# First attention: tokens as the stationary side of the scores, the mask added by VectorE

## The chip, the cores and the metric

The kernel runs on one core of a Trainium2 chip. A core has TensorE (matmuls and transposes into PSUM), VectorE, ScalarE and GpSimd for elementwise work, SyncE, and queues that start DMA transfers. The profile calls them PE, DVE, ACT, POOL and SP, and PEld is TensorE's loading of a stationary operand. The metric is the device time of one execution in microseconds (us). Before the change it is 703.99 us, the median of three runs (702.55 to 706.32).

## The reference, cut to what matters

Four batches of 1024 tokens of width 256 (x), with 77 context rows per batch, go through two layers of gated cross-attention and feed-forward. The change is in the first attention alone:

```python
def xattn(hidden, keys, values, mask):
    scores = einsum('bqd,bkd->bqk', hidden, keys)
    scores = where(mask[:, None, :] == 0, NEG_INF, scores)
    weights = softmax(scores, axis=2)
    return einsum('bqk,bkd->bqd', weights, values)

x = x + tanh(g_xattn[0]) * xattn(layernorm(x), context, context, mask)
x = x + tanh(g_ffn[0])   * (top-2 of 8 experts + shared expert)(layernorm(x))
x = x + tanh(g_xattn[1]) * second_attention(layernorm(x), context)   # softmax over the tokens
x = x + tanh(g_ffn[1])   * (gated feed-forward with int8 weights)(layernorm(x))
```

The kernel leaves layernorm out of the scores' input: since softmax doesn't change when a constant is added to a row, it uses the raw x, context rows with their mean taken off, and multiplies by the token's 1/sigma inside the exponential.

## The kernel before, in words

**Blocks.** The 4096 tokens are eight blocks `n` of 512 (two per batch), each of four token tiles of 128. The first part of the kernel works block by block in named steps. `sa:n` takes the statistics of x on VectorE (L303, L304, L306; GpSimd makes the power, L308). `a2:n` transposes x on TensorE (L333) and copies it to SBUF, one half by ScalarE and one by VectorE (L340). `context:b` takes the mean off the context rows of a batch (L265 to L269), transposes them (L272) and copies them to `cT` (L275). `a3:n` makes the scores. `a4:n` takes each token's maximum (L391, L399) and the exponentials (L403). `a5:n` transposes the probabilities (L417) and copies them (L419). `a6:n` multiplies by the context (L432) and adds to x (L438). Then come the statistics of the result (`sb`), the normalized rows on ScalarE (`nb`, L321), their transposes (`b2`), router logits (`b3`, L463), routing, ranks, and the shared expert.

**The scores before.** `a3` holds 77 context rows stationary and moves 512 tokens past them, so the scores come out with the context on the partitions (`scT`, 77 x 512). ScalarE copies them out, multiplying by 0 or 1 per context row and adding 0 or a large negative number (L379, tile `scs`). `a4` then transposes the four token tiles back on TensorE (L387), into a PSUM tile `sc` that stays taken until the four exponentials have read it.

**What sets the order.** `FIRST` is a hand-written list of steps, performed from left to right; TensorE, VectorE and ScalarE each run their instructions in exactly that order. A `.` takes the next piece of the shared expert's matmuls (L846 up, L906 down; a finished pair is evicted by ScalarE's Silu L860 and VectorE's L863), a `~` is a matmul whose result is never read (L288), a `,` starts two scatters on GpSimd (L576). The stretch around the first blocks reads

```
~ ~ ~ . ~ . ~ . ~ . . ~ sa:0 ~ a2:0 ~ context:0 ~ , sa:1 . sa:2 ~ zeros:0 a3:0 ~ ~ , a2:1 a4:0
a3:1 sa:3 a5:0 a4:1 ~ a6:0 a5:1 . a2:2 a2:3 a6:1 sb:0 context:1 nb:0 ~ biases:0 a3:2 sb:1 b2:0
a4:2 a3:3 . . . nb:1 a4:3 , a5:2 sa:4 . . . . . sa:5 . , b2:1
```

and later `weights:0 . . a3:4 a3:5 nb:2 gates:0 . a4:4 ranks:0 sb:3 . , a4:5` and `sb:4 . . nb:4 sb:5 a3:6 a3:7 . . gates:1 . a4:6`. Afterwards the routed experts run (L735 to L783), and the list `SECOND` runs the second layer.

**Tiles and loads.** PSUM has three pools: `up` (four banks: scores of `a3`, logits, shared expert, unread matmuls), `dn` (two) and `tp` (two: all transposes). SP's queue loads x in parts (L142, L145, L148), the context of batch 0 (L143) and of batches 1 to 3 (L149); ACT's queue loads the mask (L144) and the two pairs of gates (L146, L147), whose tanh (L251) is the first thing that ScalarE does.

Of the kernel before, what the change touches and what calls it, by code (L numbers as in the profile page):

```python
# [9 lines left out]
F32 = mybir.dt.float32  # L10
F32R = mybir.dt.float32r
I32 = mybir.dt.int32
U32 = mybir.dt.uint32
AF = mybir.ActivationFunctionType
ALU = mybir.AluOpType
# [3 lines left out]
P = 128  # L19
B, S, D = 4, 1024, 256  # L20
SK = 77
DC = D // P
NT = S // P
BLK = 512
TB = BLK // P
# [23 lines left out]
NEG = -(2.0**100)  # L49
# [29 lines left out]
def kernel(  # L79
# [34 lines left out]
    nc = tc.nc  # L114
    const = ctx.enter_context(tc.tile_pool(name="const", bufs=1))
# [5 lines left out]
    work = ctx.enter_context(tc.tile_pool(name="work", bufs=7))  # L121
    small = ctx.enter_context(tc.tile_pool(name="small", bufs=2))
    ps_up = ctx.enter_context(tc.tile_pool(name="ps_up", bufs=4, space=PSUM))
    ps_dn = ctx.enter_context(tc.tile_pool(name="ps_dn", bufs=2, space=PSUM))
    ps_tp = ctx.enter_context(tc.tile_pool(name="ps_tp", bufs=2, space=PSUM))

    ident = const.tile([P, P], F32, name="ident")
# [6 lines left out]


    cv = work.tile([SK, B, D], F32, tag="cv", name="cv", bufs=1)
    mask_i = const.tile([SK, B], I32, name="mask_i")
    tg_in = const.tile([P, 4], F32, name="tg_in")
    gw = const.tile([P, DC, E], F32, name="gw")
    gb = const.tile([P, 1, E], F32, name="gb")  # L140
    cv_in = context.rearrange("b k d -> k b d")
    nc.sync.dma_start(xs[0][:, : NT // 2], x_v[0][:, : NT // 2])  # L142
    nc.sync.dma_start(cv[:, 0], cv_in[:, 0])  # L143
    nc.scalar.dma_start(mask_i, mask.rearrange("b k -> k b"))  # L144
    nc.sync.dma_start(xs[0][:, NT // 2 :], x_v[0][:, NT // 2 :])  # L145
    nc.scalar.dma_start(tg_in[:, 0:2], g_xattn.partition_broadcast(P))  # L146
    nc.scalar.dma_start(tg_in[:, 2:4], g_ffn.partition_broadcast(P))  # L147
    nc.sync.dma_start(xs[1], x_v[1])  # L148
    nc.sync.dma_start(cv[:, 1:], cv_in[:, 1:])  # L149
    nc.sync.dma_start(gw, gate_w)  # L150
    nc.sync.dma_start(gb[:, 0], gate_b.partition_broadcast(P))

# [5 lines left out]
    for g in range(SH):  # L158
        for sb, src, n in zip((ws1_sb, ws3_sb, ws2_sb), (ws1, ws3, ws2), ("ws1", "ws3", "ws2")):
            t = wp.tile([P, 2, EI], F32, tag=f"{n}_{g}", name=f"{n}_{g}")  # L160
# [91 lines left out]
    tg_x0, tg_x1, tg_f0, tg_f1 = (tg[:, i : i + 1] for i in range(4))  # L252


    m01 = const.tile([SK, B], F32, name="m01")
    nc.vector.tensor_scalar(m01, mask_i, 0.0, None, ALU.not_equal)
    neg = const.tile([SK, B], F32, name="neg")
    nc.vector.tensor_scalar(neg, m01, 1.0, -NEG, ALU.subtract, ALU.mult)


    cT = const.tile([P, DC, B * SK], F32, name="cT")
# [86 lines left out]
    xT_a, score, prob, probT, ln = {}, {}, {}, {}, {}  # L348
# [16 lines left out]
    def a3(n):  # L365


        b, blk = blocks[n]
        scT = ps_up.tile([P, BLK], F32, tag="up", name=f"scT{n}")
        for dc in range(DC):  # L370
            nc.tensor.matmul(  # L371
                scT[:SK],
                lhsT=cT[:, dc, b * SK : (b + 1) * SK],
                rhs=xT_a[b][blk][:, dc],
                start=(dc == 0),
                stop=(dc == DC - 1),
            )
        score[n] = work.tile([SK, BLK], F32, tag="t2k", name=f"scs{n}")
        nc.scalar.activation(  # L379
            score[n], scT[:SK], AF.Identity, bias=neg[:, b : b + 1], scale=m01[:, b : b + 1]  # L380
        )

    def a4(n):
        scs = score.pop(n)
        sc = ps_tp.tile([P, BLK], F32, tag="tp", name=f"sc{n}")
        for tt in range(TB):
            nc.tensor.transpose(  # L387
                sc[:, tt * SK : (tt + 1) * SK], scs[:, tt * P : (tt + 1) * P], ident[:SK, :SK]
            )
        nmx = small.tile([P, TB], F32, tag="nmx", name=f"nmx{n}")  # L390
        nc.vector.tensor_reduce(  # L391
            nmx,
            sc[:, : TB * SK].rearrange("p (t k) -> p t k", k=SK),
            AX.X,
            ALU.max,
            negate=True,
        )
        rs = ln.pop(("a", n))[0]
        nc.vector.tensor_mul(nmx, nmx, rs)  # L399
        pr = work.tile([P, TB, SK], F32, tag="pr", name=f"pr{n}", bufs=2)  # L400
        sm = small.tile([P, TB], F32, tag="sm", name=f"sm{n}", bufs=4)
        for tt in range(TB):
            nc.scalar.activation(  # L403
                pr[:, tt],
                sc[:, tt * SK : (tt + 1) * SK],
                AF.Exp,
                bias=nmx[:, tt : tt + 1],
                scale=rs[:, tt : tt + 1],
                accum_out=sm[:, tt : tt + 1],
            )  # L410
        prob[n] = pr, sm
# [813 lines left out]
    def last_weights(_):  # L1225
# [6 lines left out]
        "last": last_weights,  # L1232
        "context": context_T, "zeros": lambda _: zero_rest(),
        "biases": halves_of_biases, "a2": a2, "a3": a3, "a4": a4, "a5": a5, "a6": a6,
        "b2": b2_and_shared, "b3": b3_, "routing": routing, "weights": weights,
        "ranks": ranks, "gates": gates_turned, "fetch": lambda i: combine(i // 2, i % 2),
# [104 lines left out]
```

## Time and profile before

| | us |
|---|---|
| median of three runs | 703.99 |
| the profiled execution, time | 705.87 |
| the profiled execution, span | 704.2 |
| PE busy (share of the span) | 665.7 (95%) |
| DVE busy | 382.4 (54%) |
| ACT busy | 284.4 (40%) |
| POOL busy | 276.6 (39%) |
| L371 scores, PE, 32 records | 17.7 busy |
| L387 transposes of the scores, PE, 32 records | 3.6 busy |
| L379 copy with mask, ACT, 8 | 6.1 busy |

The profile shows one execution. Its time is 1.67 us longer than its span, which begins and ends with the core's own instructions. A matmul of 32-bit floats appears as two records. Records of one engine overlap at their ends, so the distance from one start to the next, as the chain of waits gives it, says more than the length of one. The chain of waits goes back from the last instruction to what released it; the share of an engine in it is the part of the span in which nothing but that engine could have been faster. The timeline gives for each group of instructions its start, its time, and in brackets how long the engine had been idle before it and what ended that.

### The profile page before, as it was taken

The numbers are of one execution on the slowest core, as the hardware profiler recorded it, in microseconds if no ns is written. First come the engines' busy times: TensorE is split into PE (matmuls) and PEld (weight loads), VectorE is DVE, ScalarE is ACT, GpSimd is POOL, SyncE is SP. The second block draws the span as 40 slices with busy tenths as digits, with TensorE's granted clock in tenths as the row PEclk, the third lists the DMA queues.
The fourth block names the chain that finished last, engine by engine and source line by source line (L and its number), as shares of the span: only waits on it lengthen the run. The fifth ranks groups of instructions, "written<-read, shape, count | busy, mean of one in ns | idle before, by whom it ended". The sixth has DMA issues, their size and how long they took to land.

```text
span 704.2 us, 9788 instructions
## 1 busy us (share of the span) xinstructions
PE 665.7 (95%) x2996; PEld 495.8 (70%) x2996; DVE 382.4 (54%) x1096; ACT 284.4 (40%) x570; POOL 276.6 (39%) x309
## 2 busy tenths in 40 slices
PE   7689999999998999999999999999999899799896
PEld 4447487567644888888888888757767678567685
DVE  5767667566494433333343333246667559568544
ACT  1361722633221132323323233054466674666642
POOL 2111471466571133433333333231563535643642
PEclk9989999999999999999999999999999899999999
DMA  6700020121166566776776762671160004300001
GB/s 223 271 2 1 35 93 1 40 88 56 72 222 224 179 234 218 238 260 219 250 257 225 247 230 81 129 135 30 46 121 30 1 30 90 60 31 31 1 31 60
DMA packets 42259, 84.38 MB, mean 120 GB/s; under 512 B 8079, under 2 KB 12855, under 8 KB 41823
## 3 DMA queue, kind: packets, MB, share of 16 engines
q1 hardware_dynamic: 32704, 58.05, 25.0%
q0 software_dynamic: 8896, 25.70, 13.3%
q8 instruction: 24, 0.39, 0.2%
q14 instruction: 28, 0.23, 0.1%
q10 hardware_dynamic: 607, 0.00, 0.0%
HBM read 57.77 MB, written 26.87 MB: 120 GB/s over the span
## 4 chain that ended last, share of the span: by engine, by line
PE 79%; DVE 11%; ACT 5%; issue 3%; DMA 1%; POOL 1%; DVEq 0%; ACTq 0%; POOLq 0%
PE y_r L772 9%; PE pa_r L750 9%; PE pc_r L750 9%; PE y_s L906 8%; PE pa_s L846 6%; PE pc_s L846 6%; PE pa_f L1105 5%; PE pc_f L1105 5%; PE yT_f L1135 4%; PE pt_r L735 2%; PE scT L371 2%; PE sq L1014 2%; PE pl L463 2%; PE pc L1048 2%; PE pv L432 1%
## 5 line engine op out<-in xcount | busy, mean ns | idle before, releaser
L783 POOL DMA_INDIRECT yg<-yr,rowplace x74 | 72.3, 977 | 154.0 <-ACT yr L781 141.1
L1119 POOL TENSOR_TENSOR hh<-h_f,hm_f 128x512 fp32r<-128x512 f32 x47 | 63.5, 1357 | 70.2 <-DVE hm_f L1115 51.1
L762 DVE SCALAR_TENSOR_TENSOR hr<-pc_r,bt,sr 128x256 f32<-128x256 f32 (+7 forms) x78 | 32.3, 455 | 83.2 <-PE pc_r L750 83.2
L576 POOL DMA_INDIRECT xg<-rows,place x64 | 62.5, 977 | 23.0 <-issue 14.7
L772 PE MATMUL y_r<-rows_and_weights,hr 128*128 128x256 f32 (+5 forms) x296 | 70.3, 380 | 0.0
L750 PE MATMUL pa_r<-xrT,rows_and_weights 128*128 128x256 f32 (+7 forms) x312 | 69.4, 365 | 0.3 <-DVE xrT L740 0.3
L781 ACT ACTIVATE yr<-y_r,rowat 128x256 f32<-128x256 f32 (+4 forms) x74 | 31.2, 470 | 94.1 <-PE y_r L772 94.1
L750 PE MATMUL pc_r<-xrT,rows_and_weights 128*128 128x256 f32 (+7 forms) x312 | 69.1, 364 | 0.0
L846 PE MATMUL pa_s<-xnT_b,ws 128*128 128x512 f32 x128 | 62.7, 598 | 0.7 <-ACT s_s L860 0.5
L1105 PE MATMUL pa_f<-xp,ws_last 128*128 128x512 f32 x192 | 57.8, 420 | 5.7 <-POOL xp L1080 4.7
L846 PE MATMUL pc_s<-xnT_b,ws 128*128 128x512 f32 x128 | 61.8, 596 | 0.0
L750 PEld LDWEIGHTS pc_r<-xrT,rows_and_weights 128*128 128x128 f32 x312 | 56.5, 190 | 6.6
L772 PEld LDWEIGHTS y_r<-rows_and_weights,hr 128*128 128x128 f32 (+5 forms) x296 | 54.4, 186 | 8.8 <-issue 0.7
L1135 PE MATMUL yT_f<-hh,ws_last 128*128 128x512 f32 x192 | 55.9, 413 | 3.7 <-ACT hh L1123 3.0
L906 PE MATMUL y_s<-ws,hT 128*128 128x256 f32 x256 | 58.5, 380 | 0.0
L750 PEld LDWEIGHTS pa_r<-xrT,rows_and_weights 128*128 128x128 f32 x312 | 53.9, 190 | 5.7 <-DVE xrT L740 0.6
L1112 DVE SCALAR_TENSOR_TENSOR h_f<-pc_f,s_f 128x512 f32<-128x512 f32 x48 | 33.1, 689 | 38.6 <-PE pc_f L1105 19.6
L1105 PE MATMUL pc_f<-xp,ws_last 128*128 128x512 f32 x192 | 53.6, 402 | 0.3 <-DVE vw L1043 0.3
L906 PEld LDWEIGHTS y_s<-ws,hT 128*128 128x128 f32 x256 | 48.7, 191 | 7.2 <-issue 0.5
L761 ACT ACTIVATE sr<-pa_r,bt 128x256 f32<-128x256 f32 (+7 forms) x78 | 31.2, 451 | 54.5 <-PE pa_r L750 54.5
L1105 PEld LDWEIGHTS pa_f<-xp,ws_last 128*128 128x128 f32 x192 | 36.8, 194 | 17.5 <-POOL xp L1080 6.6
L740 DVE COPY xrT<-pt_r 128x512 f32<-128x512 f32 (+7 forms) x39 | 25.0, 643 | 43.1 <-PE pt_r L735 43.1
(246 smaller groups left out, 1091.2 us busy)
## 6 DMA issues: line engine op xcount, KB each, us to landing
rows_and_weights<-in_w_dram SPq DMA_DIRECT2D x117, 256.0 KB, 4.3
rows_and_weights<-xg SPq DMA_DIRECT2D x32, 272.0 KB
x<-yg POOLq DMA_DIRECT2D x16, 512.0 KB, 5.9
xg<-zero_row SPq DMA_DIRECT2D x16, 272.0 KB, 3.7
out_dram<-x SPq DMA_DIRECT2D x7, 512.0 KB, 2.6
x<-in_x_dram SPq DMA_DIRECT2D x3, 1024.0 KB
ws<-in_ws_dram SPq DMA_DIRECT2D x6, 256.0 KB, 5.7
yg<-yr,rowplace POOLq DMA_INDIRECT x74, 4.3
```

The costliest lines, as they stand in the source:

```text
L576: disjoint("xg", nc.gpsimd.indirect_dma_start(out=xg, out_offset=bass.IndirectOffsetOnAxis(ap=place[:, k, t], axis=0), in_=rows[b][:, t], ...
L750: nc.tensor.matmul(o[:, ic], lhsT=wa[:, dc, ic * P : (ic + 1) * P], rhs=xrT[:, dc], start=(dc == 0), stop=(dc == DC - 1),)
L761: nc.scalar.activation(s, ps[0][:, ic], AF.Silu, bias=bt[:, 0, ic, j])
L762: nc.vector.scalar_tensor_tensor(hr[:, ic], ps[1][:, ic], bt[:, 1, ic, j], s, ALU.add, ALU.mult)
L772: nc.tensor.matmul(o[:, tt], lhsT=hr[:, ic, tt * n : (tt + 1) * n], rhs=w[2][:, ic], start=(ic == 0), stop=(ic == IC - 1),)
L783: disjoint("yg", nc.gpsimd.indirect_dma_start(out=yg, out_offset=bass.IndirectOffsetOnAxis(ap=place[:, tt : tt + 1], axis=0), in_=y[:, tt] ...
L846: nc.tensor.matmul(ps[name], lhsT=w[g][:, dc, ic * P : (ic + 1) * P], rhs=xnTs[b][blk][:, dc], start=(dc == 0), stop=(dc == DC - 1),)
L906: nc.tensor.matmul(o[:, j], lhsT=hTs[n][i // IC][:, i % IC, cols], rhs=ws2_sb[i // IC][:, i % IC], start=False, stop=(j == 1 and i == SH * ...
L1105: nc.tensor.matmul(o, lhsT=w[:, dc, cols], rhs=halved[n][:, dc, part], start=(dc == 0 and part == 0), stop=(dc == DC - 1 and part == 1),)
L1112: nc.vector.scalar_tensor_tensor(h, pc, SCALE, s, ALU.mult, ALU.mult)
L1119: (nc.vector if end else nc.gpsimd).tensor_tensor(hh[:, 1], h, hm, ALU.subtract)
L1135: nc.tensor.matmul(y, lhsT=wd_sb[GO[i // IC]][:, i % IC, dc * P : (dc + 1) * P], rhs=hh[:, part], start=(i == 0 and part == 0), stop=(i == ...
```

## The change

`a3` now holds 128 tokens stationary and moves the 77 context rows past them: eight matmuls (four token tiles by two halves of the width) in place of two. The scores come out with the tokens on the partitions. VectorE adds the mask, broadcast over the partitions and the four tiles, and writes SBUF. The transposes in `a4` are gone, and its maximum and exponentials read SBUF. The mask is loaded once to every partition (128 x 308 integers), and one instruction makes the addend. SP's queue loads the context of batches 1 to 3 ahead of x of batch 1. The lists of steps are the same.

```diff
-    mask_i = const.tile([SK, B], I32, name="mask_i")
+    mask_i = const.tile([P, B * SK], I32, name="mask_i")
...
-    nc.scalar.dma_start(mask_i, mask.rearrange("b k -> k b"))
+    nc.scalar.dma_start(mask_i, mask.rearrange("b k -> (b k)").partition_broadcast(P))
...
+    nc.sync.dma_start(cv[:, 1:], cv_in[:, 1:])
     nc.sync.dma_start(xs[1], x_v[1])
-    nc.sync.dma_start(cv[:, 1:], cv_in[:, 1:])
...
-    m01 = const.tile([SK, B], F32, name="m01")
-    nc.vector.tensor_scalar(m01, mask_i, 0.0, None, ALU.not_equal)
-    neg = const.tile([SK, B], F32, name="neg")
-    nc.vector.tensor_scalar(neg, m01, 1.0, -NEG, ALU.subtract, ALU.mult)
+    neg = const.tile([P, 1, B * SK], F32, name="neg")
+    nc.vector.tensor_scalar(neg[:, 0], mask_i, 0.0, NEG, ALU.is_equal, ALU.mult)
...
-        scT = ps_up.tile([P, BLK], F32, tag="up", name=f"scT{n}")
-        for dc in range(DC):
-            nc.tensor.matmul(
-                scT[:SK],
-                lhsT=cT[:, dc, b * SK : (b + 1) * SK],
-                rhs=xT_a[b][blk][:, dc],
-                start=(dc == 0),
-                stop=(dc == DC - 1),
-            )
-        score[n] = work.tile([SK, BLK], F32, tag="t2k", name=f"scs{n}")
-        nc.scalar.activation(
-            score[n], scT[:SK], AF.Identity, bias=neg[:, b : b + 1], scale=m01[:, b : b + 1]
-        )
+        sc = ps_up.tile([P, BLK], F32, tag="up", name=f"sc{n}")
+        for tt in range(TB):
+            for dc in range(DC):
+                nc.tensor.matmul(
+                    sc[:, tt * SK : (tt + 1) * SK],
+                    lhsT=xT_a[b][blk][:, dc, tt * P : (tt + 1) * P],
+                    rhs=cT[:, dc, b * SK : (b + 1) * SK],
+                    start=(dc == 0),
+                    stop=(dc == DC - 1),
+                )
+        score[n] = work.tile([P, BLK], F32, tag="t2k", name=f"scs{n}")
+        nc.vector.tensor_tensor(
+            score[n][:, : TB * SK].rearrange("p (t k) -> p t k", k=SK),
+            sc[:, : TB * SK].rearrange("p (t k) -> p t k", k=SK),
+            neg[:, :, b * SK : (b + 1) * SK].to_broadcast([P, TB, SK]),
+            ALU.add,
+        )
 
     def a4(n):
-        scs = score.pop(n)
-        sc = ps_tp.tile([P, BLK], F32, tag="tp", name=f"sc{n}")
-        for tt in range(TB):
-            nc.tensor.transpose(
-                sc[:, tt * SK : (tt + 1) * SK], scs[:, tt * P : (tt + 1) * P], ident[:SK, :SK]
-            )
+        sc = score.pop(n)
```

## The prediction, made before the changed kernel ran

> **What bounds the kernel now.** I read the page first, then the chain of waits stage by stage, then the timeline and the granted clock where the chain leaves TensorE. On the page:
>
> ```profile
> PE 665.7 (95%) x2996; PEld 495.8 (70%) x2996; DVE 382.4 (54%) x1096; ACT 284.4 (40%) x570; POOL 276.6 (39%) x309
> PE 79%; DVE 11%; ACT 5%; issue 3%; DMA 1%; POOL 1%; DVEq 0%; ACTq 0%; POOLq 0%
> ```
>
> TensorE is busy for 95% of the span and carries 79% of the chain. So what leaves TensorE's order counts, unless the next thing in that order has to wait anyway. The change touches only the first 140 us. There the chain of waits has these pieces (start, length):
>
> ```profile
> 1.85 8.51 DMA tg_in<-in_g_ffn_dram
> ...
> 37.99 3.17 PE scT L371 x4
> ...
> 74.15 3.43 PE scT L371 x8
> ...
> 78.88 0.28 PE sc L387 x4
> ...
> 92.90 3.46 PE y_s L906 x16
> ...
> 97.23 1.69 PE pl L463 x16
> ```
>
> The start hangs on the gates' load. One block's scores are four records and take 1.72 us at full clock (3.43 for two) but 3.17 at 38 us; its back-transposes take 0.28. The y_s and pl rows serve to price the new matmuls. The clock behind the 3.17 is in the last column but two of the windows:
>
> ```profile
> 34.00:37.00 3.00, 0.49 (x3) 0.52 (x4) 2.19 (x9) 0.00 (x0) 1.01 (x1) 0.50 0.44 149
> 37.00:40.00 3.00, 3.00 (x5) 1.18 (x5) 2.67 (x12) 2.07 (x4) 0.00 (x0) 0.50 0.00 0
> ```
>
> TensorE idles from 32.0 to 36.5 us and is then granted half clock until 40.6; VectorE meanwhile is busy for 2.2 and 2.7 of 3 us. So up to 36.5 the chain is VectorE's. The timeline shows two places where TensorE waits for ScalarE (start, length, idle before):
>
> ```profile
> 52.11 1.13 PE L846 MATMUL pa_s<-xnT_b,ws 128*128 128x512 f32 x2
> 87.41 1.13 PE L846 MATMUL pa_s<-xnT_b,ws 128*128 128x512 f32 x2 [0.55 <-ACT s_s L860]
> ```
>
> Both are the first shared-expert matmul for which no PSUM bank is free until ScalarE has finished exponentials, loaded another table and done one Silu (s_s). At 52.11 the weight load in front of it had also waited for s_s, though TensorE itself lost only about 0.1 us. These two, and the similar pc_s at 138.07 (s_s from 137.52), decide what a shorter TensorE order is worth.
>
> **Part 1: the matmuls.** The new block has 16 records of 128 columns loaded and 77 streamed. Here a rule speaks against the change. The Trainium skill, "TensorE: Matmul & The Clock Gate", section "Part 3: Packing small matmuls — row/col tiling" (The mechanism), says that weight loads overlap matmuls in flight "only when row_grp differs", and all of these use the full array; with the same page's 128/1.2 = 107 ns per load ("LDWEIGHTS (loading the stationary operand)") and 77/512 of scT's 430 ns per record, 64 ns, of streaming, a record would take 171 ns and a block 2.74 us, 1.0 more than now. The rows say otherwise. y_s loads 128 columns for each of 16 records of 256 and takes 3.46/16 = 216 ns, which is the streaming alone (scT: 1.72/4 = 430 ns for 512 columns). pl, with 8 columns streamed, takes 1.69/16 = 106 ns, which is the load alone. So a record takes the longer of the two: 106 ns, and a block 1.69 us. I take the row: 0.03 less per block. The ends: 1.69, and 2.74 by the rule. At half clock a load-bound block would take 3.4 us, an estimate at twice 1.69.
>
> **Part 2: the back-transposes.** 8 x 0.28 = 2.2 us leave TensorE, and the `tp` bank that `sc` held is free; part of that, 0.4 us at 136.26, was a transpose waiting for the exponentials that read it.
>
> **Part 3: the mask.** ScalarE loses 8 copies of 0.77 us. VectorE gains 8 additions of 128x308. No row is that shape from PSUM; the nearest are
>
> ```profile
> L391 DVE TENSOR_REDUCE nmx<-sc 128x4 f32<-128x308 f32 x8 | 3.8, 474 | 4.7 <-PE sc L387 4.6
> L642 DVE TENSOR_REDUCE ej<-past 128x39 f32<-128x312 f32 x1 | 0.5, 468 | 0.0
> L644 DVE TENSOR_TENSOR of<-past,need 128x312 f32<-128x312 f32 x1 | 0.5, 475 | 0.0
> ```
>
> so 0.48 each, 3.8 us in all. An addition can't cost less than a pass over its elements, so there is no gain end; the upper end is the 0.68 of L1052 (128x512 from PSUM). Reading the maximum from SBUF should, by "VectorE: DVE Perf Modes", section on the SBUF-source errata (58 fixed cycles against 120 for PSUM), save 65 ns per block. The rows L642 and L391 differ by 6 ns at the same length, so I take nothing; by the rule 0.5 us of VectorE would come back. The exponentials get slower: casts from SBUF (L1123) take 612 ns, copies of the same size from PSUM (L340) 577 to 583, so 0.03 each and 0.13 per block (ends: 0 and 0.2).
>
> **Part 4: the loads.** The mask's 308 single integers become 128 rows of 1232 bytes in ACT's queue, ahead of the gates; that is 0.16 MB more, under 0.5 us at the 430 GB/s of 8 to 10 us. SP's queue gets the same instructions in another order: batch 1's x lands after 0.23 MB of context, and all of it is down by about 10.5 us, before `sa:2` (15.4 us before, about 14 after). The contexts themselves are wanted at 35 us and gain nothing. What may gain are the gates: they landed at 10.36, when the burst of x ended. I guess 7.5 to 8.5 us; ends 10.36 and 7. ScalarE then makes its table load (1.28), the tanh, and its half of the first transposes before 10.8, where VectorE's `less` ends: pt_c starts at 10.85 instead of 12.45. That is 1.6 us, and what is late next is VectorE. If the load is no earlier, this gain is zero. The mask itself is first on VectorE; landing by 5.96 as before, it delays nothing, since TensorE's unread matmuls last to 7.9.
>
> **Part 5: who waits behind the addition.** `a3` now puts an instruction on VectorE that waits for TensorE, and what follows on VectorE waits too. I follow the three stages.
>
> *13 to 33 us.* VectorE does cT, sa:1 and sa:2 (4.7 us) from 11.25, so the first addition ends at 16.7, the first copy of a2:1 starts there (19.01 before), and block 0's exponentials start at 18.3 (21.19). Block 1's addition waits for TensorE until 19.2, and sa:3 behind it ends at 22.2 (23.44). From there the order is the old one, 1.1 to 1.9 us earlier, and a6:1 ends at 31.2 to 32.0 (33.10 before). Call the end E = 31.6.
>
> *33 to 52 us.* Block 2's addition stands in front of sb:1. VectorE is ready for it at E + 7.2 (biases ended at 40.28), but the scores start at E + 4.9 (37.99 before) and need 3.4 us at half clock: the addition starts at E + 8.45. Before, sb:1 ran beside the scores; now it waits. From the addition's start it takes 0.48 + 2.4 (sb:1) + 0.7 (copy) + 0.5 + 0.3 to the exponentials, then 1.85 + 2.07 (rows of nb:1) + 1.85 + 1.28 + 0.65: TensorE gets its bank 12.1 us after the addition's start, at E + 20.55 = 52.15 against 52.11. The start's gain is eaten. If the earlier work brings the clock back at about 37 us, the scores end near 38.7 and TensorE goes on at 50.95. The middle is 51.55: -0.55 us; with E at its ends, -1.45 to +0.5.
>
> *73 to 88 us.* VectorE is full from 70.3 to 78.7. Two additions in front of nb:2 move it from 77.48 to 78.45, the rows on ScalarE from 78.36 to 78.7, and the two blocks' exponentials, with 0.26 from part 3, end at 85.6 instead of 85.17. TensorE arrives 0.6 earlier and waits 0.45 later: +0.45 (0.2 to 1.2).
>
> *122 to 140 us.* sb:5 ends at 128.3, the additions at 129.2, when gT could start anyway. The exponentials start 0.13 earlier and end 0.07 later; pc_s waits for s_s: +0.1 (0 to 0.7). The 0.4 stall at 136.26 goes, into this wait.
>
> After 140 us TensorE's order is unchanged and everything moves with it. Sum: -0.55 + 0.45 + 0.1 = 0.0 us on the profiled execution's 705.87 (704.2 of span, 1.67 around it). Against the median, 703.99, which is 0.3% lower, that is 704.0.
>
> **The rivals.** *TensorE bounds throughout* (18%): the 2.2 + 0.2 us pass to the end, and the start keeps 1.6: 704.0 - 4.0 = 700.0. For it: 95% busy. Against it: the two waits for s_s above. It needs ScalarE's chain, eased by 0.77 per block, to end earlier, which VectorE's order forbids.
>
> *VectorE's order bounds* (17%): the gates land no earlier, so E stays 33.1; the half-clock scores hold sb:1 back, +1.55 at 52; both additions and the slower exponentials come out whole at 88, 0.96 + 0.26 = +1.2; and at 138 most of the same, +0.8. That is +3.5, 707.6, slower than before. It decides from the point where the addition of block 2 starts after 40.0 us (52.11 - 12.1).
>
> *Weight loads not hidden* (6%): +1.0 for eight blocks, less 2.2 for the transposes, on top of the lost start: about 711. y_s speaks against it.
>
> *Nothing moves* (59%): as summed, 702 to 706.
>
> **How the numbers follow.** A measurement of this kernel tells about 0.5%, 3.5 us, from no change, so faster means under 700.5 and slower over 707.5. Faster: most of the first rival, 0.13. Slower: half the second, the third, and something unforeseen, 0.19. Within: 0.68. The range reaches to the first two rivals: 700.2 to 707.9.
>
> **What would show it.** Right: pt_c near 10.9; a row of 16 records per block near 1.7 us; additions near 0.48; VectorE's sb:1 starting only after block 2's addition; TensorE's first wait for s_s near 51.5 and a wait at 88 of over 1 us. Wrong: scores of over 2 us per block at full clock; pt_c still at 12.4; full clock at 34 to 41 us (then 1 us or more is gained); no wait for s_s at 88.

## The result, and the profile after

| | before | after |
|---|---|---|
| median of 22 runs each, us | 706.13 (702.26 to 709.11) | 708.50 (706.34 to 714.19) |
| ratio, with its 95% interval | | 1.0036 (1.0019 to 1.0052) |
| profiled execution: time / span, us | 705.87 / 704.2 | 707.25 / 705.5 |

The change costs 0.36%, some 2.4 us, where 0.0 was forecast. The forecast time of 704.0 and its upper end, 707.9, are missed; of the 4.5 us, 2.1 are the base, whose median is 706.13 in 22 runs and was 703.99 in the three that were known. The sets of runs below lie on two levels (the kernel before at 704 to 706 or at 738 us; in both kernels the rise comes between 100 and 300 us), so only ratios within a set are compared.

The page of the changed kernel: TensorE is as busy as before, but carries less of the chain (76% for 79%).

```profile
PE 666.4 (94%) x3060; PEld 506.6 (72%) x3060; DVE 386.1 (55%) x1103; ACT 280.1 (40%) x562; POOL 277.7 (39%) x309
PE 76%; DVE 12%; ACT 5%; issue 3%; POOL 2%; DMA 1%; DVEq 0%; ACTq 0%; POOLq 0%
```

The chain of waits (start, length), where the scores and their neighbours stand:

```profile
1.71 8.23 DMA tg_in<-in_g_ffn_dram
...
24.58 2.84 PE pv L429 x8
...
38.87 3.33 PE sc L370 x16
42.20 1.71 PE pt_b L331 x8
43.91 2.83 PE sc L370 x16
...
125.55 3.53 PE sc L370 x32
```

At 125 us two blocks of the new scores take 3.53 us, 1.77 each. The same 16 records take 3.33 at 39 us and 2.83 at 44, and the first product with the context, pv, takes 2.84 instead of the 1.73 that it takes at full clock. The windows say why (granted clock in the last column but two):

```profile
34.00:37.00 3.00, 0.00 (x0) 0.00 (x0) 2.76 (x12) 0.00 (x0) 0.60 (x1) 0.80 0.89 298
37.00:40.00 3.00, 2.61 (x11) 2.36 (x12) 2.10 (x11) 1.65 (x4) 0.41 (x1) 0.50 0.00 0
40.00:44.00 4.00, 4.00 (x21) 4.00 (x21) 2.79 (x9) 1.01 (x2) 0.00 (x0) 0.50 0.00 0
44.00:48.00 4.00, 4.00 (x20) 3.28 (x20) 3.23 (x12) 1.68 (x8) 1.01 (x1) 0.74 0.00 0
```

From 40 to 44 TensorE is busy for 4.00 of 4 us and still runs at 0.50. Windows of half a microsecond put the half clock at 11.9 to 15.3, 25.6 to 29.0 and 35.8 to 46.1 us; before it was 13.4 to 16.9 and 33.9 to 40.8. The new stretch at 25 follows a new idle time ahead of pv, where TensorE did not wait before (first TensorE's timeline in the kernel before):

```profile
24.43 1.89 PE L432 MATMUL pv<-cv,prT 77*128 77x256 f32 x8
```

VectorE's additions of the second and third block each wait for TensorE (in the changed kernel, TensorE's timeline and then VectorE's; the idle time before each in brackets):

```profile
24.58 1.99 PE L429 MATMUL pv<-cv,prT 77*128 77x256 f32 x6 [1.95 <-DVE prT L416]
53.92 1.13 PE L843 MATMUL pa_s<-xnT_b,ws 128*128 128x512 f32 x2
89.30 1.98 PE L843 MATMUL pa_s<-xnT_b,ws 128*128 128x512 f32 x4 [0.83 <-ACT s_s L857]
```

```profile
21.12 0.48 DVE L378 TENSOR_TENSOR scs<-sc,neg 128x308 f32<-128x308 f32 x1 [1.23 <-PE sc L370]
42.24 0.48 DVE L378 TENSOR_TENSOR scs<-sc,neg 128x308 f32<-128x308 f32 x1 [1.07 <-PE sc L370]
```

The two first matmuls behind a Silu come at 53.92 and 89.30, before at 52.11 and 87.41: 1.8 and 1.9 us late. So the loss of this execution is there by 54 us, and the stage to 89 adds nothing to speak of.

### The profile page after: what moved, and what is told of

The parts are those of the page before. It is cut to its first block, busy times and chain, and to the rows that moved or that the text cites. A ratio compares the mean times of both kernels' runs of the same rounds, so it can differ in the third digit from the quotient of the medians.

```text
span 705.5 us, 9907 instructions
## 1 busy us (share of the span) xinstructions
PE 666.4 (94%) x3060; PEld 506.6 (72%) x3060; DVE 386.1 (55%) x1103; ACT 280.1 (40%) x562; POOL 277.7 (39%) x309
## 4 chain that ended last, share of the span: by engine, by line
PE 76%; DVE 12%; ACT 5%; issue 3%; POOL 2%; DMA 1%; DVEq 0%; ACTq 0%; POOLq 0%
PE y_r L769 9%; PE pa_r L747 9%; PE pc_r L747 9%; PE y_s L903 8%; PE pa_s L843 6%; PE pc_s L843 5%; PE pa_f L1102 4%; PE pc_f L1102 4%; PE yT_f L1132 4%; PE pt_r L732 2%; PE sc L370 2%; PE pv L429 2%; PE pl L460 2%; PE sq L1011 2%; DVE h_f L1109 1%
## 5 line engine op out<-in xcount | busy, mean ns | idle before, releaser
L1102 PE MATMUL pa_f<-xp,ws_last 128*128 128x512 f32 x192 | 56.3, 410 | 5.3 <-POOL xp L1077 4.8
L1109 DVE SCALAR_TENSOR_TENSOR h_f<-pc_f,s_f 128x512 f32<-128x512 f32 x48 | 33.1, 689 | 37.9 <-PE pc_f L1102 20.5
```

The lines of the kernel that those rows point to most:

```text
L1102: nc.tensor.matmul(o, lhsT=w[:, dc, cols], rhs=halved[n][:, dc, part], start=(dc == 0 and part == 0), stop=(dc == DC - 1 and part == 1),)
L1109: nc.vector.scalar_tensor_tensor(h, pc, SCALE, s, ALU.mult, ALU.mult)
```

## The experiments

Four marks are read from each trace: the landing of the gates (start of ScalarE's first table load), the end of `a6:1` (E), the start of the third context's transposes (C, the first mark behind the disputed stage), and the stretches of half clock between 10 and 52 us. The marks are those of one profiled execution; the ratio is over all runs of a set (20 or 22 of most kernels in the table, six of "changed, again" and of "scores alone").

| kernel | gates | E | C | half clock, us | ratio (95%) |
|---|---|---|---|---|---|
| before | 10.43 | 33.10 | 72.07 | 3.4 + 6.8 | |
| before, again | 8.67 | 30.64 | 69.67 | 6.8 | 1.0002 (0.9984-1.0020) |
| changed | 10.01 | 33.99 | 73.89 | 3.4 + 3.4 + 10.2 | 1.0036 (1.0019-1.0052) |
| changed, again | 10.23 | 34.23 | 75.81 | 3.4 + 3.4 + 13.7 | 1.0068 (1.0041-1.0095) |
| scores alone | 10.82 | 34.83 | 76.39 | 3.4 + 3.4 + 13.7 | 1.0086 (1.0054-1.0118) |
| changed, wide fill | 10.08 | 32.71 | 71.40 | none | 1.0020 (1.0010-1.0031) |
| changed, thin fill | 10.04 | 32.33 | 71.00 | none | 1.0017 (1.0004-1.0030) |
| before, wide fill | 9.63 | 32.57 | 71.22 | none | 1.0014 (1.0004-1.0023) |

My first theory C was: the loss is TensorE's lower clock between 24 and 50 us. Its rivals were Q, that the additions hold up what is queued behind them on VectorE, and L, that the late gates and mask alone push everything back.

**Additions late (Q).** VectorE adds at the head of `a4`, behind the sums that stood behind the addition; the scores stay in their `up` bank until then.

```diff
-        score[n] = work.tile([P, BLK], F32, tag="t2k", name=f"scs{n}")
-        nc.vector.tensor_tensor(
-            score[n][:, : TB * SK].rearrange("p (t k) -> p t k", k=SK),
...
+        score[n] = sc
...
     def a4(n):
-        sc = score.pop(n)
+        b, _ = blocks[n]
+        up = score.pop(n)
+        sc = work.tile([P, BLK], F32, tag="t2k", name=f"scs{n}")
+        nc.vector.tensor_tensor(
+            sc[:, : TB * SK].rearrange("p (t k) -> p t k", k=SK),
+            up[:, : TB * SK].rearrange("p (t k) -> p t k", k=SK),
+            neg[:, :, b * SK : (b + 1) * SK].to_broadcast([P, TB, SK]),
+            ALU.add,
+        )
```

> The changed kernel with each addition of the mask issued in a4, just ahead of the maximum, in place of a3, so that nothing on VectorE stands behind an addition that waits for TensorE; the scores stay in their PSUM bank until then. Theory Q (the additions in front of sa:3 and sb:1 hold VectorE up): block 1's and 2's statistics start 1.2 and 1.1 us earlier, TensorE's wait at 54 us ends 1.0 to 2.0 us earlier, and the time falls by about that, ratio to the kernel before 1.000 to 1.002. Theory C (the longer half clock is the loss): the half-clock stretches stay, gain under 0.5 us, ratio 1.003. Theory L (the wide mask load): no gain either.

Measured: 1.0045 (1.0025 to 1.0065), E at 35.36, C at 76.88, half clock for 27 of the 41 us from 10 on. The ratio is above all that was expected. There is no gain, so Q alone doesn't carry the loss; but the clock was worse too, so this run doesn't price the additions' place.

**Idle places filled (C), and the control.** Unread matmuls of 272 columns in TensorE's idle places: five after `a2:0`, four more before `a6:0`, nine after `sb:0`; the same in the kernel before.

```diff
-~ ~ ~ . ~ . ~ . ~ . . ~ sa:0 ~ a2:0 ~ context:0 ~ , sa:1 . sa:2 ~ zeros:0 a3:0 ~ ~ , a2:1 a4:0
-a3:1 sa:3 a5:0 a4:1 ~ a6:0 a5:1 . a2:2 a2:3 a6:1 sb:0 context:1 nb:0 ~ biases:0 a3:2 sb:1 b2:0
+~ ~ ~ . ~ . ~ . ~ . . ~ sa:0 ~ a2:0 ~ ~ ~ ~ ~ ~ context:0 ~ , sa:1 . sa:2 ~ zeros:0 a3:0 ~ ~ , a2:1 a4:0
+a3:1 sa:3 a5:0 a4:1 ~ ~ ~ ~ ~ a6:0 a5:1 . a2:2 a2:3 a6:1 sb:0 ~ ~ ~ ~ ~ ~ ~ ~ ~ context:1 nb:0 ~ biases:0 a3:2 sb:1 b2:0
```

> The changed kernel with unread 272-column matmuls put where TensorE idles: 5 more in front of pt_c of batch 0, 4 more in front of block 0's pv, 9 in front of pt_c of batch 1. Theory C: full clock from 12 to 46 us; pv 1.7 us in place of 2.84, block 2's scores 1.7 in place of 3.3, block 3's 1.7 in place of 2.8; 2 to 4 us gained, ratio 0.997 to 1.001. Theory Q: the clock comes back, but block 2's addition then waits for VectorE's biases (1.1 us earlier than now at most), gain about 1.0, ratio 1.002. Theory L: no gain.

> The kernel before with the same unread matmuls at the same three places, as a control. Theory C: it has half clock at 13.3 to 16.8 and 34.0 to 40.6 us too, so it gains, but less than the changed kernel, 1 to 2 us (ratio 0.997 to 0.9985). Theory Q: block 2's statistics don't wait for the scores here, so the gain is under 0.7 us (ratio 0.999 or more).

Windows of the filled changed kernel:

```profile
20.00:24.00 4.00, 3.69 (x18) 2.56 (x18) 3.49 (x12) 1.00 (x6) 0.76 (x1) 1.00 0.92 357
24.00:28.00 4.00, 3.22 (x18) 2.44 (x18) 3.02 (x9) 2.43 (x9) 0.24 (x1) 1.00 0.06 16
28.00:36.00 8.00, 7.38 (x38) 5.87 (x36) 6.37 (x20) 0.59 (x1) 0.87 (x1) 1.00 0.89 285
36.00:46.00 10.00, 9.03 (x55) 6.51 (x56) 7.79 (x29) 4.84 (x14) 1.14 (x2) 1.00 0.07 23
```

The clock is full throughout. With the gates no earlier (10.08), E is 1.3 us earlier than in the changed kernel and C 2.5 us, and 4.4 against the changed kernel of the next set. The two filled kernels, run side by side, differ by 0.0006, within either interval. That alone doesn't make the change free at full clock, since the fill is in the way in the control. TensorE's timeline at the first product with the context, first in the kernel before as it ran again (no fill, full clock until 31 us), then in the control, then in the changed kernel with the thin fill described below:

```profile
21.96 1.89 PE L432 MATMUL pv<-cv,prT 77*128 77x256 f32 x8
```

```profile
21.85 2.50 PE L288 MATMUL unread<-zero_row,ones_sq 128*128 128x272 f32 x10
24.18 1.89 PE L432 MATMUL pv<-cv,prT 77*128 77x256 f32 x8
```

```profile
23.75 1.99 PE L436 MATMUL pv<-cv,prT 77*128 77x256 f32 x8 [0.21 <-DVE prT L423]
```

Counted from the first context's transposes (at 11.29, 11.66 and 12.06), pv comes after 10.7, 12.5 and 11.7 us, and E after 19.4, 20.9 and 20.3. In the control, pv stands right behind ten records of fill; in the changed kernel TensorE is through with its fill and waits for VectorE. So at full clock the change still costs about 1 us up to E, and the filled control hides it. From E to C both filled kernels take 38.7 us; there the change costs nothing at full clock.

The traces are as theory C had them and the times are not: 1.0020 lies above its 0.997 to 1.001, and the control's 1.0014 above its 0.997 to 0.9985. Filling the kernel before gains nothing and costs 0.14%, so the fill is a probe here, no improvement.

**Gates first (L).** The gates' two loads ahead of the mask's on ACT's queue, the addend made by a step of its own just before `a3:0`.

```diff
-    nc.scalar.dma_start(mask_i, mask.rearrange("b k -> (b k)").partition_broadcast(P))
...
     nc.scalar.dma_start(tg_in[:, 0:2], g_xattn.partition_broadcast(P))
     nc.scalar.dma_start(tg_in[:, 2:4], g_ffn.partition_broadcast(P))
+    nc.scalar.dma_start(mask_i, mask.rearrange("b k -> (b k)").partition_broadcast(P))
...
+    def mask_added(_):
+        nc.vector.tensor_scalar(neg[:, 0], mask_i, 0.0, NEG, ALU.is_equal, ALU.mult)
```

> The changed kernel with the gates' two loads ahead of the mask's in ACT's queue and the mask's addend made just before block 0's scores, not first on VectorE. Theory L: the gates land by 8 us in place of 10, pt_c starts near 11.0 in place of 12.0, VectorE's statistics no longer wait for the mask at 6.9; 1.0 us gained (ratio 1.002), all of it seen at the end of a6:1 (33.0 in place of 34.0). Theories Q and C: what is gained at 12 us is waited for again by 54 us, gain under 0.4 (ratio 1.003 or more).

```profile
7.80 1.28 ACT L251 ACT_TABLE_LOAD   x1 [7.80 <-DMA tg_in<-in_g_ffn_dram]
```

The gates land 2.2 us earlier and E comes 1.0 earlier (32.95), but half clock lasts 3.4 + 13.7 us, C is at 74.79, and the ratio 1.0038 (1.0024 to 1.0053), where theory L had 1.002: the start's gain is gone by 75 us. L alone is not the loss.

**The changed kernel again, one part alone, three mended, thin fill.** The second kernel is the one before with only the two loads exchanged, as the change has it; the third has gates first, additions late and the wide fill; the fourth has the fill in matmuls of 77 columns (8 and 18):

```diff
+    def thin():
+        o = ps_up.tile([P, BLK], F32, tag="up", name="unread_thin")
+        nc.tensor.matmul(
+            o[:, :77], lhsT=ones_sq, rhs=zero_row[:, 0, :77], start=True, stop=True
+        )
...
-a3:1 sa:3 a5:0 a4:1 ~ a6:0 a5:1 . a2:2 a2:3 a6:1 sb:0 context:1 nb:0 ~ biases:0 a3:2 sb:1 b2:0
+a3:1 sa:3 a5:0 a4:1 ~ = = = = = = = = a6:0 a5:1 . a2:2 a2:3 a6:1 sb:0 = = = = = = = = = = = = = = = = = = context:1 nb:0 ~ biases:0 a3:2 sb:1 b2:0
```

> The changed kernel itself, unaltered, so that the other three stand beside it on one chip. All theories: 1.0036 times the kernel before (1.002 to 1.005), as the first measurement. Its profile should again have half clock between about 36 and 46 us and TensorE's wait for the first gated context ending near 54; if the half clock is elsewhere in this execution and the wait moves with it, that speaks for theory C (the clock).

> The kernel before with one part of the change alone: the other batches' context is asked for ahead of the second block of tokens. Theory C (clock) and theory Q (the addition ahead of the sum of the second batch): the part is worth nothing, 0.999 to 1.001, since both loads have landed before anything waits for them. Rival: the second block of tokens lands later and its transposes come later, so that TensorE idles once more before 20 us: then the end of the first attention's second block is over 33.5 us (33.10 before) and the ratio over 1.001.

> The changed kernel with the gates' two loads ahead of the mask's, the additions at the head of the softmax (behind the sums that TensorE waits for), and unread 272-column matmuls in TensorE's three idle places. Theory C: end of the first attention's second block at 31.7 to 32.7, TensorE's wait for the first gated context over by 50 to 51.5, and the whole 0.996 to 1.000 of the kernel before, as what is saved at 52 us is 1 to 2 us of 704 less what comes back later. Rival G (what is gained early is given back later, at the waits after 55 us that are bound by the chain of VectorE and ScalarE): the wait is over by 51.5, and the ratio is still 1.000 to 1.002.

> The changed kernel with TensorE's idle places filled by unread matmuls of 77 columns (26 of them) in place of those of 272 columns. If thin matmuls count as work for the clock as wide ones do: full clock from 20 to 50 us and the wait for the first gated context over by 52, as with the wide ones (51.4). If they don't: half clock stays at 25 to 28 and at 36 to 46 us, and the wait ends at 53 or later.

The changed kernel: 1.0068, over the 1.002 to 1.005 expected, with half clock from 36.3 to 49.9 us, one stretch more than in its first profile, and C 1.9 us later than there; TensorE no longer waits for the Silu at all, its own slowed order is last. The half clock and TensorE's arrival at that point moved together, which speaks for theory C. The exchange alone: 0.9987 (0.9976 to 0.9998), a little below the 0.999 to 1.001 expected, gates at 8.81, E at 30.35. Three mended: 1.0031 (1.0020 to 1.0042), gates at 7.93 but E at 33.24; half clock fell on the fill itself (20.5 to 23.9), whose ten records took 3.54 us there. The place was overfilled, and the ratio lies above both expectations. Thin fill: 1.0017, the clock full throughout. From 31.05 to 35.19 us TensorE runs 36 records of the thin fill, and with two wide ones and a block's transposes between them two blocks' scores, and the clock stays full. So matmuls of 77 columns keep a full clock, as the wide ones do.

**Scores alone, the wide mask alone, order and fill, before again.** The scores without the exchange; the kernel before with the exchange and an unread mask on 128 partitions ahead of the gates (the mask that is read behind them); the exchange with nine wide fills after `sb:0`; the kernel before.

```diff
-    nc.scalar.dma_start(mask_i, mask.rearrange("b k -> k b"))
...
+    nc.scalar.dma_start(wide, mask.rearrange("b k -> (b k)").partition_broadcast(P))
     nc.scalar.dma_start(tg_in[:, 0:2], g_xattn.partition_broadcast(P))
     nc.scalar.dma_start(tg_in[:, 2:4], g_ffn.partition_broadcast(P))
+    nc.scalar.dma_start(mask_i, mask.rearrange("b k -> k b"))
...
```

> The change without the exchange of the two loads: the new scores and the addition, the other batches' context behind the second block of tokens as before. Theory M (the mask, asked for on all 128 partitions ahead of the gates, holds the gates back and eats what the earlier context gives): the gates land at 10.5 to 12 us (9.94 in the changed kernel, 10.36 before), the end of the first attention's second block is at 34.5 to 36, and the ratio to before is 1.004 to 1.012. Rival: the exchange of the loads does nothing for the changed kernel either: gates at 9.9, ratio 1.004 to 1.007 as the changed kernel itself.

> The kernel before with the two loads exchanged (0.9987 alone) and, ahead of the gates on ScalarE's queue, an unread load of the mask on 128 partitions (the narrow one that is read comes behind the gates, and what is made of it is made after the fourth block's sums). Its scores are those of before. Theory M: gates land at 9.7 to 10.3 (8.8 at most with the exchange alone), the end of the second block is at 31.8 to 33.2 in place of 30.35, and the ratio 1.000 to 1.002. Rival (the gates' landing is set by other loads): gates at 8.3 to 8.9 and the ratio 0.998 to 0.9995.

> The kernel before with the two loads exchanged and nine unread 272-column matmuls in TensorE's longest idle place (after the second batch's sum). Theory C (the clock): no half clock at 31 to 38, block 2's scores in 1.72 us in place of 3.1, TensorE's wait for the first gated context over at 48 to 49.3 (49.42 with the exchange alone), ratio 0.996 to 0.9985. Rival (the wait is set by VectorE's chain and not by TensorE's clock, and the fill costs what it gains): 49.4 or later, ratio 0.9985 to 1.000.

> The kernel before itself, unaltered, so that its profile stands beside the others on this chip: ratio 1.000 (0.999 to 1.001); gates at 10.4, end of the first attention's second block at 33.1, wait for the first gated context over at 52.1, with half clock in two or three stretches between 13 and 41 us. If its gates land near 8.8 on this chip, the exchange of the loads is not what brought them forward in the run with the exchange alone.

Scores alone: 1.0086 from six runs, in theory M's range, though its interval (1.0054 to 1.0118) reaches into the rival's. The wide mask in the kernel before: gates at 9.39, between the two expectations; E at 32.06 and 1.0000 (0.9983 to 1.0018), as theory M had them. Order and fill: 0.9991 (0.9977 to 1.0006), gates at 9.62, no half clock at 31 to 38, C at 70.96. That is the rival's range. E to C takes 38.7 us here, with TensorE waiting 0.33 us for ScalarE's Silu, and 39.0 in the unfilled kernel: the 6.8 us of half clock cost the kernel before some 0.4 us there, as another chain is last. And the kernel before, unaltered, had this:

```profile
8.67 1.28 ACT L251 ACT_TABLE_LOAD   x1 [8.67 <-DMA tg_in<-in_g_ffn_dram]
```

Its gates land at 8.67 here and at 10.43 in its first profile. By what I had written down, the exchange is then not what brought them to 8.81; whether it moves them at all stays open (10.82 without it and 10.0 with it in the changed kernel is one execution against several). In kernels with the narrow mask ahead of the gates they landed at 8.67 to 10.43 (five traces), with the wide one ahead of them at 9.39 to 11.10 (ten), with the gates first at 7.80 to 7.96 (five, of either kernel).

**Wide or thin matmuls ahead of the third block's scores.** 14 unread matmuls of 272 columns or 32 of 77 columns between `biases:0` and `a3:2`, where TensorE has just been idle and goes on without a pause.

```diff
-a3:1 sa:3 a5:0 a4:1 ~ a6:0 a5:1 . a2:2 a2:3 a6:1 sb:0 context:1 nb:0 ~ biases:0 a3:2 sb:1 b2:0
+a3:1 sa:3 a5:0 a4:1 ~ a6:0 a5:1 . a2:2 a2:3 a6:1 sb:0 context:1 nb:0 ~ biases:0 ~ ~ ~ ~ ~ ~ ~ ~ ~ ~ ~ ~ ~ ~ a3:2 sb:1 b2:0
```

> The changed kernel with 14 unread 272-column matmuls right ahead of the third block's scores, at the end of TensorE's idle place (some 6.4 us of work at half clock). Theory W (matmuls of 77 columns don't bring the clock back, wide ones do): the clock is full again within two stretches of 3.4 us from the first of them, by 42 to 44.5 us, and the third block's scores take 1.7 to 2.2 us. Rival (phase only): the same as with the thin ones of the next run, within one stretch.

> The same place and about the same work at half clock (some 6.6 us), in 32 unread matmuls of 77 columns. Theory W: the clock stays at half through the thin ones and through the scores behind them, past 47 us, and the third block's scores take 3.3 us. Rival (phase only): full by 42 to 45 us, scores in 1.7 to 2.2 us.

Windows of the kernel with the wide ones (they run from 41.1 to 49.6):

```profile
40.70:44.11 3.41, 3.41 (x9) 2.66 (x10) 2.65 (x11) 2.07 (x4) 0.00 (x0) 0.50 0.00 0
44.11:49.40 5.29, 5.29 (x24) 4.37 (x23) 0.29 (x1) 0.00 (x0) 0.00 (x0) 1.00 0.00 0
```

Windows, and then the chain, of the one with the thin ones:

```profile
39.76:44.00 4.24, 4.24 (x22) 4.24 (x20) 2.19 (x9) 1.74 (x4) 0.00 (x0) 0.50 0.00 0
44.00:49.00 5.00, 5.00 (x25) 5.00 (x25) 0.00 (x0) 0.00 (x0) 0.00 (x0) 0.50 0.00 0
...
53.33:56.74 3.41, 3.41 (x18) 3.41 (x17) 0.00 (x0) 0.00 (x0) 0.00 (x0) 0.50 0.02 5
...
61.00:65.00 4.00, 4.00 (x10) 2.25 (x10) 1.15 (x4) 3.94 (x13) 0.00 (x0) 0.59 0.00 0
```

```profile
39.96 13.57 PE unread_thin L291 x64
53.53 3.41 PE sc L377 x16
56.94 1.71 PE pt_b L338 x8
58.65 3.33 PE sc L377 x16
61.98 2.99 PE pa_s L850 x4
```

Behind the wide ones the clock is full after one stretch of 3.41 us. Through the thin ones, two blocks' scores and a block's transposes it stays at half for 22 us of uninterrupted work, and comes back at 64.3, 2.3 us into the shared expert's 512-column matmuls; the whole stretch is 27.3 us, eight times 3.41. (One execution each: 751 and 758 us, where the kernel before takes 738; the fill is in the way.) Theory W holds in these two traces: the thin records keep a full clock but don't bring it back. Whether it is the few columns or the weight load in front of each that makes the difference was not isolated. One exception stands: in the first profile of the changed kernel the clock came back at 46.1, within the scores, after three stretches.

**Two candidates.** The kernel before with the gates' loads first; the changed kernel with the gates first and a thin fill (6 and 18). In both, what VectorE makes of the mask comes just before `a3:0` and no longer first.

```diff
-    nc.scalar.dma_start(mask_i, mask.rearrange("b k -> k b"))
...
     nc.scalar.dma_start(tg_in[:, 0:2], g_xattn.partition_broadcast(P))
     nc.scalar.dma_start(tg_in[:, 2:4], g_ffn.partition_broadcast(P))
+    nc.scalar.dma_start(mask_i, mask.rearrange("b k -> k b"))
...
```

> The kernel before with the gates' two loads ahead of the mask's on ScalarE's queue. From the runs so far the third context's transposes start 61.7 us after the gates' landing, as long as the first context's own transposes (11.0 to 11.7 us) don't hold more back: gates at 7.8, those transposes at 11.0 to 11.7, so 68.8 to 70 us for the third context's, in place of 69.7 to 72.1 before: ratio 0.996 to 0.9995. Rival (what is gained early is given back at later waits): 0.9995 to 1.001.

> The changed kernel with the gates' loads first and TensorE's two idle places filled with 24 unread matmuls of 77 columns. Theory C: clock full from 20 to 56 us, end of the second block at 30.3 to 31.5, third context's transposes at 69 to 70.3, ratio 0.996 to 0.9995: it then beats the changed kernel by 0.4 to 0.8% and is level with the kernel before with its gates first. Rival: half clock comes in spite of the fill, or the fill is in the way: third context at 71 or later, ratio over 1.000.

The first: 0.9984 (0.9973 to 0.9995), the lowest ratio of all kernels here, though its interval overlaps that of the exchange alone. The second: 1.0018 (1.0007 to 1.0029), the rival's range, though its gates land at 7.93, as the other's do at 7.88, and its clock is full. The two are the cleanest pair for the additions' place: both have full clock until 35 us and the first context's transposes at 11.8. VectorE's timeline, first of the kernel before with gates first, then of the changed one, and the changed one's pv on TensorE:

```profile
21.85 0.68 DVE L421 COPY prT<-pt_p 77x512 f32<-77x512 f32 x1
```

```profile
20.42 0.48 DVE L387 TENSOR_TENSOR scs<-sc,neg 128x308 f32<-128x308 f32 x1 [1.23 <-PE sc L379]
...
23.14 0.68 DVE L425 COPY prT<-pt_p 77x512 f32<-77x512 f32 x1
```

```profile
23.88 1.99 PE L438 MATMUL pv<-cv,prT 77*128 77x256 f32 x8 [0.67 <-DVE prT L425]
```

The second block's addition holds VectorE idle for 1.23 us, the fourth block's sums wait behind it, and the copy that TensorE's pv needs comes 1.29 us later; E is 0.85 later (32.47 against 31.62) and C 1.2 (71.51 against 70.34). TensorE is through with its fill and waits 0.67 us for that copy, so it isn't the fill that holds pv. So Q is real where the clock is full. The two ratios differ by 0.0034, 2.5 us, of which the traces show 1.2 at C; the fill stands ahead of C, so its price is in that, and where the rest comes from is not shown.

**Additions late, with the thin fill.** The thin fill with late additions, without and with the gates first.

> The changed kernel with its idle places filled with thin unread matmuls, as in the run that gave 1.0017, and the additions moved to the head of the softmax, behind the sums that stood behind them. Theory Q2 (with the clock full, the addition's wait on VectorE is the rest of the loss): the second block ends at 31.2 to 31.9 instead of 32.33, the third context's transposes start at 68.8 to 70.3 instead of 71.0, ratio 0.998 to 1.0005. Rival (the rest is elsewhere, and the additions only move): 32.1 to 32.6 and 70.7 to 71.5, ratio 1.001 to 1.0025.

> The same with the gates' loads ahead of the mask's and the mask's addend made just ahead of the first addition. Theory Q2: the second block ends at 30.6 to 31.6, the third context's transposes at 68.3 to 70, ratio 0.9965 to 0.9995, so faster than the changed kernel by 0.5% or more and level with or ahead of the kernel before with its gates first (0.9984). Rival: 71 or later, ratio 1.0005 to 1.0025.

1.0048 (1.0023 to 1.0073) and 1.0039 (1.0016 to 1.0063): above both expectations, so theory Q2's remedy gains nothing. A view of TensorE's waits in the first:

```profile
PE unread L286 <- DVE scs L390: 0.7, 1, 0.7
```

The scores that wait for a later addition keep their `up` bank, and TensorE waits for the bank. And the clock was not full: the first has half clock from 13.2 to 20.2 us, ahead of any fill, and from 23.6 to 34.0, with E at 39.62. The sixteen thin records of the fill take 3.33 us there and don't bring the clock back; it comes back 5.2 us after them, during the transposes behind the wider pv. Over this kernel's runs the time goes from 703.35 (mean clock 0.994) to 713.43 (0.977). In the second kernel, the six runs with a mean clock of 0.992 or more took 702.6 to 703.6 us, and the seven of the kernel before at 0.989 or more 701.2 to 703.7. So these two runs don't price the late addition at full clock; what they show is that it doesn't keep the clock full.

## Why the prediction was wrong

Two steps failed: Part 4's gain at the start, and in Part 5 the granted clock: no half clock was reckoned with ahead of pv, and behind it none past the third block's scores. The first block pair ended at E = 33.99 in place of 31.6, half of that from each step.

**Part 1 (matmuls)** held: 1.76 to 1.77 us per block at full clock, no 2.74. Its half-clock estimate, 3.4, held too (3.33). What it didn't see is that these matmuls prolong the half clock.

**Part 3 (mask)** held: additions 0.47 each, the maximum 0.463 from SBUF against 0.474 from PSUM (11 ns, not the 65 of the rule that it had set aside); the exponentials rose by 0.027, 0.03 forecast:

```profile
L400 ACT ACTIVATE pr<-scs,nmx,rs_a 128x77 f32<-128x77 f32 x32 | 14.0, 440 | 9.2 <-DVE nmx L396 9.2
...
L388 DVE TENSOR_REDUCE nmx<-scs 128x4 f32<-128x308 f32 x8 | 3.7, 463 | 0.0
L378 DVE TENSOR_TENSOR scs<-sc,neg 128x308 f32<-128x308 f32 x8 | 3.6, 470 | 2.8 <-PE sc L370 2.8
```

**Part 4 (loads)** failed at "I guess 7.5 to 8.5 us": the gates landed at 10.01, and pt_c started at 12.04 instead of 10.85. The first profile's late 10.36 was taken as the rule of the kernel before; its other execution had 8.67. "Landing by 5.96 as before, it delays nothing" also failed: the mask landed by 6.88 and VectorE's first sums began 1.0 later. Price at E: 1.2 us, the delay of pt_c.

**Part 5, 13 to 33 us**, failed by another 1.2 us: E came 21.95 us after pt_c where the steps gave 20.75. With the clock held full it came 20.3 to 20.7 after, so the steps were right at full clock, and the term left out was this: behind the additions TensorE idles 1.95 us before pv, and half clock follows. The steps were also compared with an execution of the kernel before that had half clock itself (13.4 to 16.9, E 20.65 after pt_c); at full clock up to 31 us that kernel needs 19.4. So the forecast had the additions nearly free where they cost about 1 us.

**33 to 52 us.** The chain held in kind: the addition started at E + 8.25 (8.45 forecast), TensorE went on at E + 19.9 (19.95 to 20.55). But the half clock, for which I weighed "if the earlier work brings the clock back at about 37 us", went the other way, to 46 or 50. In the first profile, with three stretches, C comes at E + 39.9; in the executions with four, TensorE itself is last and C comes at E + 41.6. In the kernel before it is E + 39.0, and 38.7 in either filled kernel. That the first profile's E + 19.9 meets the forecast is in part luck: at half clock to 46 us, TensorE's own order got there within about 0.1 us of ScalarE's chain, and one stretch more shows in full (41.6 for 39.9, half of 3.41).

**73 to 88 and 122 to 140 us** were over-priced: +0.45 came out as +0.07 (1.89 late at the Silu wait, 1.82 at C), and +0.1 as -0.46 (pv after 140 us is 1.42 late, the third context's successor at 123.46 was 1.88 late): the 0.4 us stall on the exponentials that Part 2 named did vanish there. The wait at 88 of over 1 us that was to show the forecast right came as 0.83. Part of the over-pricing is a reading: the exponentials before end at 85.35 in the trace, not at 85.17.

Sum in the profiled executions: 1.82 + 0.07 - 0.46 = 1.4 of the measured 1.38 us. The median's 2.4 would hold executions with a longer half clock; that is argued from the mean clock, with which the changed kernel's 22 times fall by 3.6 us per 0.01. Two sets list the clock of both kernels: the median is 0.952 for the changed kernel again against 0.960 before, and 0.9735 for the scores alone against 0.982. At the kernel before's own 3.2 and 3.6 us per 0.01 in these sets, that is an estimated 2.6 of 4.7 us and 3.0 of 6.1, so about half of the loss goes with the clock. Of the rivals, "VectorE's order bounds" came nearest: its deciding point (the third block's addition after 40.0) was passed at 42.24 and its +1.55 at 52 came as +1.8, but what it added at 88 and 138 did not come.

What stays open: the 0.17 to 0.20% by which the changed kernel is slower with the clock held, some 1.3 to 1.5 us. The additions' place on VectorE has that size (about 1 us up to E), and with the thin fill TensorE waits for VectorE there and not for its fill. But the one remedy tried, the late additions, brought a wait of its own and a worse clock, so this share is argued and not isolated.

## What to carry to other kernels

Where TensorE idles for some microseconds and then starts on matmuls that are bound by their weight loads, price them at half clock, and the work behind them too, until wide matmuls come. But ask what is last there: 6.8 us of half clock cost the kernel before only some 0.4 us, since another chain was last. Turning one operand around can be free by the sum of its records and still cost this. An instruction that waits for another engine holds everything behind it in its own queue, and moving it later holds a buffer instead: price both. And read the landing of a load that starts the chain from more than one execution before building on it, and put the load that others wait for first in its queue: the gates then landed at 7.8 to 8.0 us, which was worth 0.16% in the kernel before and nothing that shows in the changed one.

## What the runs showed of the hardware

The half clock comes in stretches of 3.41 us and their multiples, up to eight. That agrees with the Trainium skill, "TensorE: Matmul & The Clock Gate", Part 1, What's actually happening, which gives a window of about 3.4 us and says that one busy window brings the full clock. With wide matmuls it did (one stretch, then 1.00). With matmuls of 77 columns and a weight load each (and one block's transposes among them) it didn't for 22 us of unbroken work, and the measurement decides: by the page the clock would have been back after the first stretch of unbroken work, at 42.6 us in the changed kernel's first profile and 43.1 in its second; it came at 46.1 and 49.9. At full clock the same thin matmuls hold it. Also not expected: the gates' landing differs by 1.8 us between two executions of one kernel (8.67 and 10.43).
